# GpSimd takes a second of four products with C in every other group of a selective scan

## Chip, cores and metric

One core of one Trainium2 chip runs the whole program in one launch. The metric is the device time of one execution in microseconds. Before the change three runs took 1963.19, 1964.97 and 1970.44 us; the median is 1964.97.

## What is computed

The reference adds four branches to x (4 batches of 512 tokens of width 512): a quantized two-layer block, a feed-forward with weights from a 16-entry table, a selective scan (Mamba) that is gated by x, and a routed mixture of 32 experts. Only the scan is touched here. Cut to it:

```python
dt = softplus(dt_low @ dt_proj_w + dt_proj_b)     # one value for each channel and step
A = -exp(A_log)                                   # 512 channels x 16 states

def step(state, inp):
    d, b, c, u = inp
    dA = exp(d[..., None] * A)
    state = state * dA + (d * u)[..., None] * b[:, None, :]
    y = einsum('bdn,bn->bd', state, c)
    return state, y
```

For each of 512 channels and 16 states there is a recurrence over 512 steps. Its states are multiplied with C and summed over the 16 states.

## The kernel before

**Stages.** Three stretches follow each other. Up to 345 us: the quantized block, the table lookups that make the feed-forward weights, and the first batch's preparation of the scan. From 345 to about 1103 us: scan and feed-forward, batch by batch. After it: the experts. In the middle stretch the function `weave` (L1052) draws steps from several generators in proportion to their number: the scan of batch b (`scan`, L538), the feed-forward (`lut_ffn`, L352), the preparation of batch b+1 (`prepare`, L481) and the routing of batch b-1 (`route`, L689). This fixes the order in which instructions are written down. A scheduler then orders them for each engine by its own estimate of when inputs and buffers are there, and every engine runs its own list strictly in order.

**Tiles of the scan.** A tile has 128 partitions, 16 states times 8 channels, and 512 steps. For every batch, block of 128 channels `e` (4) and `v` (4) there is one *group* of four tiles, `j` from 0 to 3. So there are 64 groups (16 for each batch) and 256 tiles. I number the groups from 0 to 63; groups with odd number have v = 1 or 3. For each tile:

- SyncE issues a load of `d` (L556; dt and dt times u, spread over 16 states; 4 buffers).
- ScalarE makes the decay, exp(A dt), into a PSUM bank `st` (L561; 3 banks).
- GpSimd makes `dBu`, dt times u times B (L563; 3 buffers).
- VectorE runs the recurrence, `tensor_tensor_scan` (L566 for j = 0, L568 for the others).
- The states are multiplied with C, the second half of the tile `BC`, into a tile `sc` (5 buffers of 128x512 in SBUF).

The last step is where j matters. For j = 0 the scan writes `sc` in SBUF directly, and GpSimd multiplies it in place (L573), written down behind the dBu of j = 2 by `issue_after`, which adds an edge in GpSimd's own order and no wait on another engine. For the other three the scan writes back to its PSUM bank, and VectorE multiplies from there into `sc` (L569).

After the fourth tile, TensorE sums over states with four matmuls (L579), one for each j, into 32 partitions of the bank `py`. Tile 3 goes first, the other three behind it. They free the four `sc` buffers. After four groups VectorE adds the skip term (L589).

**What stands around it.** TensorE's list holds the feed-forward matmuls (L375 gate and up, L391 down) between the groups. VectorE closes each feed-forward chunk with L384 and L385, which free the PSUM bank of that chunk, and adds L391's result to x at L398. `prepare` uses GpSimd for four products of each block (L530, L532, L533, L534) and a store (L535), and VectorE for the convolution (L500, L504) and L529. Layer norms have VectorE statistics (L101, L102, L103), a power on GpSimd (L104) and VectorE's L106, which waits for it. `route` has the matmuls L705 and L710 and the small ones L780, L781 and L819, with VectorE's L782, L801 and L808 beside them.

Of the kernel before, what the change touches and what calls it, by code (L numbers as in the profile page):

```python
# [22 lines left out]
ALU = mybir.AluOpType  # L23
# [36 lines left out]
class Kernel:  # L60
# [477 lines left out]
    def scan(self, mp, b):  # L538


        nc = self.nc
        skip = self.vecs[:, 2, :]
        u = self.u[b]
        BC = mp.tile([P, 2, S], F32, tag="BC", name="BC", bufs=1)
        for g in range(2):
            nc.sync.dma_start(
                out=BC[:, g, :], in_=self.xdbl[b, 1 + g].unsqueeze(1).to_broadcast([NST, CPT, S])
            )
        for e in range(KH):
            py = self.bank("y", f"py{e}")  # L550
            for v in range(4):
                scs = []
                for j in range(4):
                    r0 = e * P + 32 * j + CPT * v
                    d = mp.tile([P, 2, S], F32, tag="d", name="d", bufs=4)
                    nc.sync.dma_start(  # L556
                        out=d, in_=self.dts[b, r0 : r0 + CPT].unsqueeze(0).to_broadcast([NST, CPT, 2, S])
                    )
                    st = self.bank("d", "st")
                    i = (e * 4 + v) * 4 + j  # L560
                    nc.scalar.activation(st, d[:, 0, :], AF.Exp, scale=self.A[:, i : i + 1])  # L561
                    dBu = mp.tile([P, S], F32, tag="dBu", name="dBu", bufs=3)
                    product = nc.gpsimd.tensor_tensor(dBu, d[:, 1, :], BC[:, 0, :], ALU.mult)  # L563
                    sc = mp.tile([P, S], F32, tag="sc", name="sc", bufs=5)
                    if j == 0:
                        nc.vector.tensor_tensor_scan(sc, st, dBu, 0.0, ALU.mult, ALU.add)  # L566
                    else:
                        nc.vector.tensor_tensor_scan(st, st, dBu, 0.0, ALU.mult, ALU.add)  # L568
                        nc.vector.tensor_tensor(sc, st, BC[:, 1, :], ALU.mult)  # L569
                    scs.append(sc)  # L570
                    if j == 2:
                        with self.tc.issue_after(product.ins):
                            nc.gpsimd.tensor_tensor(scs[0], scs[0], BC[:, 1, :], ALU.mult)  # L573
                    if j < 3:
                        yield

                with ExitStack() as behind:
                    for j in (3, 0, 1, 2):
                        y = nc.tensor.matmul(  # L579
                            py[32 * j : 32 * j + 32, :],  # L580
                            lhsT=self.sum_states[:, v, :],
                            rhs=scs[j],
                            start=v == 0,
                            stop=v == 3,
                        )
                        if j == 3:
                            behind.enter_context(self.tc.issue_after(y.ins))
                yield
            nc.vector.scalar_tensor_tensor(  # L589
                u[:, e, :], u[:, e, :], skip[:, e : e + 1], py, ALU.mult, ALU.add  # L590
            )
# [598 lines left out]
```

## Time and profile before

| what | value |
|---|---|
| median of three runs | 1964.97 us (1963.19 to 1970.44) |
| profiled execution, its time | 1967.59 us |
| profiled execution, its span | 1965.8 us |
| mean granted clock of TensorE | 0.933 |
| busy over the span: PE, DVE, ACT, POOL | 85%, 61%, 36%, 51% |
| scan stretch, 345 to 1103 us: PE, DVE, ACT, POOL busy | 660.76, 673.06, 345.83, 503.67 us |
| one product with C: on DVE (L569), on POOL (L573) | 681, 1300 ns |
| one scan (L566, L568) | 1214, 1218 ns |

PE is TensorE's matmul, DVE is VectorE, ACT is ScalarE, POOL is GpSimd and SP is SyncE. The profile is of one execution. Times are microseconds unless marked ns. A row of a group names the source line, the engine, the operation, the tiles written and read, the count, then busy time and the mean of one, then the idle time of the engine just before, with what ended it. A row of the waits reads: who waited, for what, how long in all, how often, and the longest. A row of the timeline has start, duration, engine, line, and in brackets the idle time before it. How much is busy over the whole span is an average over stretches with different limits; the table therefore gives the scan stretch on its own.

### The profile page before, as it was taken

The numbers are of one execution on the slowest core, as the hardware profiler recorded it, in microseconds if no ns is written. First come the engines' busy times: TensorE is split into PE (matmuls) and PEld (weight loads), VectorE is DVE, ScalarE is ACT, GpSimd is POOL, SyncE is SP. The second block draws the span as 40 slices with busy tenths as digits, with TensorE's granted clock in tenths as the row PEclk, the third lists the DMA queues.
The fourth block names the chain that finished last, engine by engine and source line by source line (L and its number), as shares of the span: only waits on it lengthen the run. The fifth ranks groups of instructions, "written<-read, shape, count | busy, mean of one in ns | idle before, by whom it ended". The sixth has DMA issues, their size and how long they took to land. (4 is left out here: it accounts for less than half of the span.)

```text
span 1965.8 us, 25002 instructions
## 1 busy us (share of the span) xinstructions
PE 1667.2 (85%) x8845; PEld 984.2 (50%) x8845; DVE 1192.7 (61%) x2029; ACT 712.7 (36%) x1345; POOL 999.0 (51%) x824
## 2 busy tenths in 40 slices
PE   4778775899889888888799688799999999999980
PEld 2444332556454545454555344455556566556540
DVE  6887864788799979999889634422222233222231
ACT  1554455535443554355433322222222222222210
POOL 3110113768755875478566543556555555555420
PEclk9889986899999998899999799999999999999985
DMA  9524510889887888788789686688888877877656
GB/s 264 140 80 153 182 50 34 221 201 227 211 234 165 208 212 213 165 200 205 207 198 221 189 210 134 165 180 197 176 181 178 185 164 160 180 169 170 111 128 186
DMA packets 187673, 346.69 MB, mean 176 GB/s; under 512 B 41698, under 2 KB 88130, under 8 KB 187540
## 3 DMA queue, kind: packets, MB, share of 16 engines
q1 hardware_dynamic: 147332, 251.96, 48.6%
q0 software_dynamic: 39952, 92.66, 23.7%
q8 instruction: 72, 1.18, 0.3%
q10 hardware_dynamic: 256, 0.39, 0.1%
q14 instruction: 61, 0.50, 0.1%
HBM read 277.08 MB, written 76.32 MB: 180 GB/s over the span
## 5 line engine op out<-in xcount | busy, mean ns | idle before, releaser
L968 POOL DMA_INDIRECT sums<-ey,to x168 | 260.8, 1552 | 311.5 <-DMA sums<-ey,to 123.4
L925 PE MATMUL pg<-exT,egu 128*128 128x320 f32 (+1 forms) x1536 | 402.5, 419 | 15.5 <-DVE eh L943 7.6
L563 POOL TENSOR_TENSOR dBu<-d,BC 128x512 f32<-128x512 f32 x256 | 330.8, 1302 | 112.1 <-DMA d<-dts 79.8
L925 PEld LDWEIGHTS pg<-exT,egu 128*128 128x128 f32 x1536 | 289.2, 191 | 131.8 <-issue 38.0
L568 DVE TENSOR_TENSOR_SCAN st<-st,dBu 128x512 f32<-128x512 f32 x192 | 230.7, 1218 | 29.9 <-POOL dBu L563 25.3
L561 ACT ACTIVATE st<-d,A 128x512 f32<-128x512 f32 x256 | 173.5, 689 | 189.9 <-DVE sc L569 122.1
L375 PE MATMUL pgu<-xT,wg 128*128 128x256 f32 (+1 forms) x704 | 189.4, 412 | 30.6 <-DVE h L385 26.1
L900 POOL DMA_INDIRECT xg<-xln,tokens x168 | 162.0, 964 | 90.8 <-issue 37.9
L942 DVE SCALAR_TENSOR_TENSOR eh<-eh,pg 128x320 f32<-128x320 f32 (+5 forms) x144 | 61.1, 425 | 230.6 <-ACT eh L941 229.3
L954 PE MATMUL po_e<-ed,eh 128*128 128x512 f32 (+1 forms) x336 | 172.9, 633 | 13.2 <-ACT ey L967 6.2
L340 PE MATMUL pw<-oh,lut_t 128*32 128x344 bf16 (+1 forms) x2052 | 127.0, 359 | 65.5 <-DVE oh L334 65.2
L375 PEld LDWEIGHTS pgu<-xT,wg 128*128 128x128 f32 (+1 forms) x704 | 132.3, 198 | 97.3 <-DVE h L385 39.0
L375 PE MATMUL pgu<-xT,wu 128*128 128x256 f32 (+1 forms) x704 | 179.4, 397 | 0.0
L967 ACT ACTIVATE ey<-po_e,gates 128x512 f32<-128x512 f32 (+1 forms) x104 | 68.8, 684 | 303.8 <-PE po_e L958 151.1
L965 DVE TENSOR_SCALAR ey<-po_e,gates 128x512 f32<-128x512 f32 x64 | 45.9, 748 | 209.0 <-PE po_e L958 209.0
L391 PE MATMUL po_f<-wd,h 128*128 128x512 f32 (+1 forms) x352 | 159.8, 610 | 2.6 <-DVE h L385 2.2
L375 PEld LDWEIGHTS pgu<-xT,wu 128*128 128x128 f32 (+1 forms) x704 | 138.5, 199 | 25.8 <-issue 2.9
L569 DVE TENSOR_TENSOR sc<-st,BC 128x512 f32<-128x512 f32 x192 | 127.7, 681 | 19.8 <-PE py L579 18.9
L573 POOL TENSOR_TENSOR sc<-sc,BC 128x512 f32<-128x512 f32 x64 | 83.2, 1300 | 110.0 <-DVE sc L566 83.1
L958 PE MATMUL po_e<-ed,eh 64*128 64x512 f32 (+1 forms) x336 | 114.8, 638 | 0.0
L340 PEld LDWEIGHTS <-lut_t 128*32 128x32 bf16 x2052 | 56.3, 102 | 113.2 <-issue 74.0
L391 PEld LDWEIGHTS po_f<-wd,h 128*128 128x128 f32 (+1 forms) x352 | 68.0, 196 | 86.3 <-issue 80.6
(260 smaller groups left out, 2195.0 us busy)
## 6 DMA issues: line engine op xcount, KB each, us to landing
d<-dts SPq DMA_DIRECT2D x256, 512.0 KB, 6.3
egu<-in_w_gate SPq DMA_DIRECT2D x40, 384.0 KB, 3.8
ix<-idx_b SPq DMA_DIRECT2D x16, 688.0 KB, 5.4
egu<-in_w_up SPq DMA_DIRECT2D x40, 256.0 KB, 5.2
ed<-in_w_down SPq DMA_DIRECT2D x40, 256.0 KB, 4.0
ed<-in_w_down SPq DMA_DIRECT2D x80, 128.0 KB, 4.5
sums<-zero SPq DMA_DIRECT2D x12, 768.0 KB, 6.7
dts<-dt POOLq DMA_DIRECT2D x16, 512.0 KB, 4.5
```

Of the source, the lines that this page charges most:

```text
L340: nc.tensor.matmul(pt[i][32 * c : 32 * c + 32, :step], lhsT=self.lut_t[:, j, g, :], rhs=oh[:, c * n + i * step : c * n + (i + 1) * step], ...
L375: nc.tensor.matmul(pg[:m, j * W : (j + 1) * W], lhsT=w[:, k, c * P : c * P + m], rhs=xT[:, k, :], start=k == 0, stop=k == KH - 1,)
L391: nc.tensor.matmul(po, lhsT=h[:m, c, i * P : (i + 1) * P], rhs=self.wd[:m, c, :], start=c == 0, stop=c == NIC - 1,)
L561: nc.scalar.activation(st, d[:, 0, :], AF.Exp, scale=self.A[:, i : i + 1])
L563: product = nc.gpsimd.tensor_tensor(dBu, d[:, 1, :], BC[:, 0, :], ALU.mult)
L568: nc.vector.tensor_tensor_scan(st, st, dBu, 0.0, ALU.mult, ALU.add)
L569: nc.vector.tensor_tensor(sc, st, BC[:, 1, :], ALU.mult)
L900: nc.gpsimd.indirect_dma_start(out=xg[:m, :], out_offset=None, in_=xln, in_offset=bass.IndirectOffsetOnAxis(ap=tokens[:m, lo + j, col : co ...
L925: nc.tensor.matmul(pg[i][:, :hs], lhsT=w[:, k, i * P : (i + 1) * P], rhs=xT[:, k, z : z + hs], start=k == 0, stop=k == KH - 1,)
L954: nc.tensor.matmul(po[j][:m, :], lhsT=h[:, 0, b : b + m], rhs=wd[:, 0, :], start=True, stop=False)
L958: nc.tensor.matmul(po[j][:m, :], lhsT=h[r : r + R, 1, b : b + m], rhs=wd[r : r + R, 1, :], start=False, stop=True)
L968: nc.gpsimd.indirect_dma_start(out=sums[j], out_offset=bass.IndirectOffsetOnAxis(ap=to[:m, lo + j, col : col + 1], axis=0), in_=y[:m, :], ...
```

## The change

In groups with odd v, `share` is 2: the scans of tiles 0 and 1 both write `sc` directly, and GpSimd multiplies both in place, that of tile 0 behind the dBu of tile 2 as before and that of tile 1 behind the dBu of tile 3. In these groups the summing matmuls begin with tile 1, then 3, 0 and 2. Groups with even v stay as they were. Counted over the program, 32 of the 192 products of VectorE go, and GpSimd has 96 instead of 64.

```diff
             for v in range(4):
-                scs = []
+
+                share = 1 + v % 2
+                products, scs = [], []
                 for j in range(4):
...
-                    product = nc.gpsimd.tensor_tensor(dBu, d[:, 1, :], BC[:, 0, :], ALU.mult)
+                    products.append(nc.gpsimd.tensor_tensor(dBu, d[:, 1, :], BC[:, 0, :], ALU.mult))
                     sc = mp.tile([P, S], F32, tag="sc", name="sc", bufs=5)
-                    if j == 0:
+                    if j < share:
                         nc.vector.tensor_tensor_scan(sc, st, dBu, 0.0, ALU.mult, ALU.add)
                     else:
                         nc.vector.tensor_tensor_scan(st, st, dBu, 0.0, ALU.mult, ALU.add)
                         nc.vector.tensor_tensor(sc, st, BC[:, 1, :], ALU.mult)
                     scs.append(sc)
-                    if j == 2:
-                        with self.tc.issue_after(product.ins):
-                            nc.gpsimd.tensor_tensor(scs[0], scs[0], BC[:, 1, :], ALU.mult)
+                    if 2 <= j < 2 + share:
+                        with self.tc.issue_after(products[j].ins):
+                            nc.gpsimd.tensor_tensor(scs[j - 2], scs[j - 2], BC[:, 1, :], ALU.mult)
                     if j < 3:
                         yield
 
                 with ExitStack() as behind:
-                    for j in (3, 0, 1, 2):
+                    order = (3, 0, 1, 2) if share == 1 else (1, 3, 0, 2)
+                    for j in order:
                         y = nc.tensor.matmul(
...
-                        if j == 3:
+                        if j == order[0]:
                             behind.enter_context(self.tc.issue_after(y.ins))
```

## What I expect

> **What bounds the kernel now.** I read the windows view first, cut where the scan begins (345 us) and ends (1103 us). Its columns are busy time and instructions of each engine, the granted clock, the DMA share and GB/s.
>
> ```profile
> core 0: us, PE busy (x) PEld busy (x) DVE busy (x) ACT busy (x) POOL busy (x), PEclk, DMA share, GB/s
> 345.00:1103.00 758.00, 660.76 (x3028) 404.15 (x3032) 673.06 (x1025) 345.83 (x558) 503.67 (x408) 0.94 0.83 204
> 1103.00:1966.00 863.00, 764.92 (x3089) 450.80 (x3081) 268.55 (x553) 209.55 (x545) 424.67 (x338) 0.95 0.76 171
> ```
>
> The change touches only the first stretch. There two engines are almost full: VectorE 673 of 758 us (89%) and TensorE 661 (87%). GpSimd has 254 us free. The waits of VectorE in that stretch (who waited for whom: us, times, longest) say what its 85 idle us are:
>
> ```profile
> DVE st L568 <- POOL dBu L563: 25.3, 18, 4.2
> DVE sc L569 <- PE py L579: 18.9, 18, 2.6
> DVE ln_off L106 <- POOL ln_rs L104: 12.6, 9, 2.2
> ```
>
> Call a group's instructions b0 to b3 (dBu, L563), S0 to S3 (scans, L566 and L568), M (product with C on VectorE, L569), C (the same on GpSimd, L573) and y (the four summing matmuls, L579). The first wait is an S for its b. The second is M1 for a free sc buffer, which a y of the group before holds. TensorE comes to that y late: in the timeline the median y starts some 3 us after its last M, with feed-forward matmuls before it. One such place, S3 of group 24 and then M1, which waits until the y of group 23 end (640.12 + 1.06 us):
>
> ```profile
> 638.34 1.22 DVE L568 TENSOR_TENSOR_SCAN st<-st,dBu 128x512 f32<-128x512 f32 x1
> 641.20 0.69 DVE L569 TENSOR_TENSOR sc<-st,BC 128x512 f32<-128x512 f32 x1 [1.64 <-PE py L579]
> ```
>
> I followed the waits back by hand from the last M (1102.5 us): where an engine had no gap, to its instruction before; where it had one, to the releaser. Of the 757 us some 340 lie on VectorE, 250 on TensorE, 80 on GpSimd, 55 on DMA (d loads, BC, xln) and 20 on ScalarE. So VectorE's time is worth its full price on less than half of the way. Of the 32 M1 that the change removes (groups with odd v), 16 lie on a VectorE piece (groups 9, 15, 25, 27, 31, 41, 43, 45, 47, 49, 53, 55, 57, 59, 61, 63), the other 16 where TensorE, GpSimd or a transfer decides.
>
> **What is removed and added.** From the page:
>
> ```profile
> L568 DVE TENSOR_TENSOR_SCAN st<-st,dBu 128x512 f32<-128x512 f32 x192 | 230.7, 1218 | 29.9 <-POOL dBu L563 25.3
> L569 DVE TENSOR_TENSOR sc<-st,BC 128x512 f32<-128x512 f32 x192 | 127.7, 681 | 19.8 <-PE py L579 18.9
> L573 POOL TENSOR_TENSOR sc<-sc,BC 128x512 f32<-128x512 f32 x64 | 83.2, 1300 | 110.0 <-DVE sc L566 83.1
> ```
>
> Removed: 32 M1, 32 x 0.681 = 21.8 us of VectorE's records; back to back they overlap a little (two in 1.28 us), so 0.64 each on a full engine, 20.5 us. Added: 32 C1 on GpSimd, 32 x 1.30 = 41.6 us, which raises it from 504 to 545 of 758. S1 now writes SBUF instead of PSUM: L566 does that at 1214 ns against 1218, nothing. Loads, exps and matmuls keep their numbers.
>
> **What the built order adds to the diff.** S1 writes sc itself, so what waited for the sc buffer was M1 and is now S1, a scan earlier. The instruction order of the built kernel shows two answers. In 14 of the 32 groups (3, 5, 7, 9, 13, 21, 25, 29, 37, 41, 45, 53, 57, 61 of 0 to 63) the scheduler puts S1 behind S3: S0 S2 S3 S1 M2 M3; in group 11 it stands between S2 and S3. In the other 17 the order is kept, in several of them with two y of the group before pulled ahead of a block of feed-forward matmuls. C1 mostly stands before the next group's b2, which needs a dBu buffer that S1 frees anyway, so it adds a length but hardly a new wait.
>
> A moved S1 costs in this way. After S0 GpSimd does C0 and b3, and S3 can't start before:
>
> ```profile
> 1027.80 1.27 POOL L573 TENSOR_TENSOR sc<-sc,BC 128x512 f32<-128x512 f32 x1 [0.53 <-DVE sc L566]
> 1029.03 1.26 POOL L563 TENSOR_TENSOR dBu<-d,BC 128x512 f32<-128x512 f32 x1
> ```
>
> S0 of that group ends at 1027.7, b3 at 1030.3, S3 starts at 1030.32: 2.6 us, against 2 x 1.17 = 2.34 for S1 and S2 between. In the moved order only S2 (and what else falls there) fills the 2.6 us, S3 starts no earlier, and S1 (1.17) follows where M1 (0.64) stood: **0.53 us later, not 0.64 sooner**. The same 0.53 is lost where S1, instead of M1, starts at TensorE's gate.
>
> **The sum on the path** (times of before, order of after):
> - kept order on a VectorE piece (groups 27, 43, 49, 59, 63): 5 x 0.64 = 3.2 sooner. Group 55, freed of its gate, gives 0.3 before TensorE's own backlog decides.
> - groups 21 and 37: L398, for which TensorE waits (6.75 us once, as "PE pl L710 <- DVE x L398"), comes ahead of S1; with C1 and the early y behind it, I count 0.7 and 1.9 sooner.
> - moved on a VectorE piece: 45, 53, 61 lose 0.53 each (1.6); 57 0.65; 9 0.9 (a feed-forward product falls behind S3 too); 25 and 41 come out even, since other work is pulled before their gate.
> - groups 15, 31, 47: the last C1 stands ahead of the pow of L104, for which L106 waits 2.2 us each time. It adds 1.24 and saves 0.64: 0.6 lost, three times, 1.8.
> - group 11: C1 joins a GpSimd piece (461 to 484 us): 1.25 lost. Elsewhere GpSimd's own waits for d (79.8 us) and for S0 (83.1 us) hide C1; without that cover all 32 would cost 41.6 us.
> - the 16 off VectorE pieces that are not named: nothing.
>
> Sooner 6.1, later 6.2.
>
> **A rule against it.** One row stands out among VectorE's groups in the scan stretch:
>
> ```profile
> L504 DVE SCALAR_TENSOR_TENSOR u<-u,acc 128x512 f32<-128x512 f32 x12 | 11.5, 955 | 0.1
> ```
>
> Its shortest takes 671 ns in the trace, the mean 955, the longest 1740, which is one GpSimd product more. The Trainium skill ("SBUF — State Buffer", Who interferes with whom) says that such an instruction and a GpSimd one that reads SBUF exclude each other for the whole instruction, and that one with at most one SBUF input does not contend. M1 read PSUM and one SBUF tile, so the rule makes the swap bad: VectorE gives up an uncontended product and GpSimd holds the port 41.6 us more. If every new C1 held such an instruction for half its length, 32 x 0.65 = 21 us. The row says less: the scans keep 1198 to 1234 ns beside GpSimd throughout, and what stands over the shortest is (955-671) x 12 = 3.4 us for L504 and about 1.6 for L604, with some more in L529 and L801; call it 8 us for a GpSimd busy 66%. At 72% it grows by 8/66 x 6 = 0.7 us. I take 0.7, bounded by 0 and 21.
>
> Total: 6.9 later, 6.1 sooner, **0.8 us later**. The profiled execution took 1967.59 (span 1965.8), 2.6 over the median 1964.97. So 1968.4 for it and about 1966 for a median.
>
> **Rivals.**
> 1. *Faster: the freed VectorE time counts.* For it: 89% busy, and TensorE waits for h (26.1 us) and py for sc (10.9), which an earlier VectorE shortens. The 16 on its path give 16 x 0.64 = 10.2, with groups 21 and 37 12.8: 1952. All 32 would give 1944, which the TensorE pieces exclude. Against it: the 14 moved scans.
> 2. *Slower: TensorE waits for C1.* y of an odd group now begins with tile 1, and TensorE is in order: the feed-forward matmuls stand behind it, VectorE's L384 and L385 behind those. At the groups' ends C1 should come near the last M. In groups 11, 27, 29, 43 and 45 prep products (L530 to L534, 1.27 each) stand ahead of it. If C1 comes 3 us after the last M everywhere, the odd groups at which TensorE is less than 3.7 us behind (3, 11, 17, 25, 27, 35, 43, 49, 57, 59, 63) lose 14 us together: 1979. It decides from about 2 us of lateness; at 0 it costs nothing. For it: each b between C1 and its S1 is 1.3 us. Against it: TensorE is 4 to 10 us behind in most odd groups.
> 3. *Slower by the port*, 21 us: 1986. Unlikely by the scans' steady times.
>
> **Chances.** No measurable change 0.62, rival 1 0.14, rivals 2 and 3 and other sums of lost waits 0.24. What a measurement of this kernel can tell from no change is 0.5%, 9.8 us: below 1955.1 or above 1974.8. Each piece is a count of small, alike terms (0.5 to 2 us) of both signs, so the likeliest case alone spans 1957 to 1974. The range reaches to rivals 1 and 2: 1953 to 1980.
>
> **What would show it.** VectorE's busy time in the scan stretch falls by some 20 us and GpSimd's rises by some 41, yet the stretch stays within a few us of 758. Waits of S for dBu grow (25.3 to 35 or more), as do those of L106 for L104 (12.6 by 3 to 4); what waited as M1 for y appears as a scan that waits for y. L569 falls to 160 rows at 681 ns. Wrong would be: a stretch 10 us shorter with unchanged waits (VectorE was the bound), py waiting for the C product on GpSimd by over 10 us (rival 2), or scans or L504 longer on average (rival 3).

## The result and the profile after

The changed kernel took **1991.30 us** (median of 4 runs, 1990.54 to 1992.80), beside 1964.08 us for the kernel before on the same chip. The medians are 27 us apart. The ratio of the record is 1.0126, with a 95% interval of 1.0105 to 1.0148: 25 us slower, where no measurable change was forecast, and outside the range.

The windows view of the kernel after, cut where its scan ends (columns as in the forecast):

```profile
core 0: us, PE busy (x) PEld busy (x) DVE busy (x) ACT busy (x) POOL busy (x), PEclk, DMA share, GB/s
345.00:1134.00 789.00, 685.55 (x3032) 409.19 (x3032) 662.14 (x993) 344.73 (x558) 538.63 (x439) 0.93 0.80 196
1134.00:1990.00 856.00, 763.19 (x3081) 452.38 (x3081) 268.61 (x553) 209.61 (x545) 424.31 (x338) 0.95 0.77 173
```

The whole loss lies in the scan. The window of before, in the forecast, ends ahead of the last group's y; up to the end of that y (1104.5 us) TensorE has 662.2 us and VectorE 673.2. Between equal ends the stretch grew by 29.5 us (759.5 to 788.9). What follows it was untouched and took 861 us before and 856 after; over the traces of all kernels here it took 853 to 869. VectorE has 32 products fewer and is 11 us less busy. **TensorE is 23 us busier with the same matmuls**, and the other 6 us are added idle time on it.

The costliest groups of the page after (lines from L554 on stand two or three further down than before; L570 and L568 are the scans, L571 the product with C on VectorE, L575 that on GpSimd):

```profile
L575 POOL TENSOR_TENSOR sc<-sc,BC 128x512 f32<-128x512 f32 x96 | 124.4, 1296 | 116.6 <-DVE sc L568 93.9
L570 DVE TENSOR_TENSOR_SCAN st<-st,dBu 128x512 f32<-128x512 f32 x160 | 192.5, 1217 | 61.3 <-POOL dBu L565 46.1
L571 DVE TENSOR_TENSOR sc<-st,BC 128x512 f32<-128x512 f32 x160 | 105.7, 677 | 18.0 <-PE py L582 17.3
```

Scan and product have kept their lengths (1217 and 677 ns against 1218 and 681). What grew on VectorE is the waiting. The waits of the same kernel, in the scan stretch:

```profile
DVE st L570 <- POOL dBu L565: 46.1, 32, 3.6
...
PEld py L582 <- POOL sc L575: 17.7, 7, 4.8
...
PE py L582 <- POOL sc L575: 15.0, 6, 4.6
...
DVE ln_off L106 <- POOL ln_rs L104: 9.8, 9, 2.2
...
DVE sc L568 <- PE py L582: 8.7, 11, 2.3
```

The wait of the scans for dBu grew as foreseen (25.3 to 46.1), and 8.7 us of the waits for y are now those of scans, as foreseen too. The one for L104 fell (12.6 to 9.8) where it was to grow. The second and third line are new, and are one wait seen twice, at the weight load and at the matmul: **TensorE stands still at a summing matmul for GpSimd's product**. In the trace 14.6 us of it lie in four places. 2.75 us from 608.8, 4.56 from 816.3 and 3.37 from 1021.0 us are in groups 21, 37 and 53, all three among the 14 with a moved scan; 3.91 from 1126.9 are in group 63, the last, whose order of scans is unchanged; there TensorE was idle before as well, for 5.78 us until VectorE's last product. This is the first of them, in the timeline:

```profile
606.42 1.23 DVE L570 TENSOR_TENSOR_SCAN st<-st,dBu 128x512 f32<-128x512 f32 x1 [1.23 <-POOL dBu L565]
...
608.19 0.66 PE L708 MATMUL pt_r<-ident,xn_r 128*128 128x128 f32 x4
...
608.38 0.68 DVE L398 TENSOR_TENSOR x<-x,po_f 128x512 f32<-128x512 f32 x1
...
608.98 1.22 DVE L568 TENSOR_TENSOR_SCAN sc<-st,dBu 128x512 f32<-128x512 f32 x1
...
610.27 1.27 POOL L575 TENSOR_TENSOR sc<-sc,BC 128x512 f32<-128x512 f32 x1 [0.57 <-DVE sc L568]
...
611.60 1.48 PE L582 MATMUL py<-sc,sum_states 128*32 128x512 f32 x2 [2.75 <-POOL sc L575]
```

Read it from below. TensorE is in order, and its list has the y of tile 1 ahead of the routing's matmuls (L713). These could start at 609.5 us: L398 has by then read the PSUM bank that they write (609.1; it is one of two banks that L391, L708 and L713 share), and ScalarE has their input (L710, 609.5). The y waits until 611.6 for C1, C1 for S1, and S1 stands behind S3, which itself waited 1.23 us for b3, and behind L398. Tile 1 is first in y, but its product is the last thing of its group to be ready.

This wait is not all added time. In groups 21 and 37 the kernel before was idle at the same place, 3.39 and 6.75 us in front of the routing's matmul, until L398 freed the bank. Its waits had this line, which the kernel after does not have:

```profile
PE pl L710 <- DVE x L398: 10.1, 2, 6.8
```

The other loss of TensorE is seen in the rest of group 21's y (629.20), in those of group 22, in two parts, and in those of group 23. Each y makes two records, so x8 are four matmuls:

```profile
629.20 1.06 PE L582 MATMUL py<-sc,sum_states 128*32 128x512 f32 x6
630.66 0.66 PE L366 MATMUL pt_x<-ident,xn 128*128 128x128 f32 x4 [0.40 <-ACT xn L111]
632.28 1.05 PE L582 MATMUL py<-sc,sum_states 128*32 128x512 f32 x4 [0.97 <-DVE sc L571]
...
636.92 1.05 PE L582 MATMUL py<-sc,sum_states 128*32 128x512 f32 x4
...
648.77 1.06 PE L582 MATMUL py<-sc,sum_states 128*32 128x512 f32 x8
```

**Four y side by side take 1.06 us, three take 1.06, and two 1.05.** A group whose y are parted by other matmuls pays that for each part. The order built for the kernel before parts 4 of the 64 groups, that for the change 15. The time with a y on TensorE went from 75.9 to 93.6 us, 17.7 of the 23 us above. Eleven more parts at 1.05 us are 11.6 of them. The other 6 are y that ran at half the granted clock, of which there are more after:

```profile
562.50 1.92 PE L582 MATMUL py<-sc,sum_states 128*32 128x512 f32 x4 [0.42 <-DVE sc L571]
```

The windows view has a granted clock of 0.50 for these 1.92 us and of 1.00 for the 1.06 us at 648.77. In all traces here the record of the granted clock has only 1.0 and 0.5 in this stretch. Half of the time in which TensorE is busy at 0.5 can thus be counted as lost by the clock, and the rest of its busy time as work. So counted, from the trace of before to that of after, with the places bounded by the ends of the groups' y:

| place | longer, us | work | lost at half clock | idle |
|---|---|---|---|---|
| ends of batches: from group 11 to 15, 27 to 31, 43 to 48, 55 to 60 | 20.9 | 1.9 | 12.2 | 6.8 |
| groups 20 to 23, 36 to 39, 52 to 55 | 8.2 | 6.6 | 0.4 | 1.3 |
| the rest of the stretch | 0.4 | 2.7 | -0.5 | -2.0 |
| all, 345 us to the last y | 29.5 | 11.2 | 12.1 | 6.1 |

The work is the parted y. Around groups 21, 37 and 53 these, not the idle time, make most of the loss against the kernel before. The larger loss lies at the ends of the batches, where GpSimd prepares the next batch, and most of it is TensorE at half clock. Each side is one execution, and no run sets the clock by itself; what lowers it is left open.

### The profile page after: what moved, and what is told of

It is laid out like the page before. It is cut to its first block, busy times and chain, and to the rows that moved or that the text cites. A ratio compares the mean times of both kernels' runs of the same rounds, so it can differ in the third digit from the quotient of the medians.

```text
span 1989.5 us, 24948 instructions
## 1 busy us (share of the span) xinstructions
PE 1689.4 (85%) x8836; PEld 990.8 (50%) x8845; DVE 1181.7 (59%) x1997; ACT 711.8 (36%) x1345; POOL 1033.7 (52%) x856
## 5 line engine op out<-in xcount | busy, mean ns | idle before, releaser
L570 DVE TENSOR_TENSOR_SCAN st<-st,dBu 128x512 f32<-128x512 f32 x160 | 192.5, 1217 | 61.3 <-POOL dBu L565 46.1
L375 PE MATMUL pgu<-xT,wg 128*128 128x256 f32 (+1 forms) x704 | 194.3, 421 | 26.0 <-DVE h L385 23.7
L575 POOL TENSOR_TENSOR sc<-sc,BC 128x512 f32<-128x512 f32 x96 | 124.4, 1296 | 116.6 <-DVE sc L568 93.9
L957 PE MATMUL po_e<-ed,eh 128*128 128x512 f32 (+1 forms) x336 | 172.3, 632 | 13.6 <-ACT ey L970 6.2
L375 PE MATMUL pgu<-xT,wu 128*128 128x256 f32 (+1 forms) x704 | 175.0, 389 | 0.0
L391 PE MATMUL po_f<-wd,h 128*128 128x512 f32 (+1 forms) x352 | 161.7, 615 | 5.2 <-DVE h L385 3.5
L568 DVE TENSOR_TENSOR_SCAN sc<-st,dBu 128x512 f32<-128x512 f32 x96 | 116.4, 1213 | 11.0 <-PE py L582 8.7
L571 DVE TENSOR_TENSOR sc<-st,BC 128x512 f32<-128x512 f32 x160 | 105.7, 677 | 18.0 <-PE py L582 17.3
L391 PEld LDWEIGHTS po_f<-wd,h 128*128 128x128 f32 (+1 forms) x352 | 68.4, 197 | 90.6 <-issue 82.1
```

Source lines behind the costliest of these rows:

```text
L375: nc.tensor.matmul(pg[:m, j * W : (j + 1) * W], lhsT=w[:, k, c * P : c * P + m], rhs=xT[:, k, :], start=k == 0, stop=k == KH - 1,)
L391: nc.tensor.matmul(po, lhsT=h[:m, c, i * P : (i + 1) * P], rhs=self.wd[:m, c, :], start=c == 0, stop=c == NIC - 1,)
L575: nc.gpsimd.tensor_tensor(scs[j - 2], scs[j - 2], BC[:, 1, :], ALU.mult)
L957: nc.tensor.matmul(po[j][:m, :], lhsT=h[:, 0, b : b + m], rhs=wd[:, 0, :], start=True, stop=False)
```

## The experiments

At first there were three theories. *S*: tile 1 first in y parts the summing matmuls. *G*: 32 more products on GpSimd cost something although it has idle time. *M*: the 14 scans moved behind the fourth. Ratios are to the kernel before on the same chip; 0.001 is 2 us. "Parted" and "moved" count groups in the built order. What is told of a place in a trace comes from one execution.

| run | what | parted | moved | ratio (95%) |
|---|---|---|---|---|
| after | the change | 15 | 14 | 1.0126 (1.0105 to 1.0148) |
| b_y1first | before, with the new order of y | 14 | 0 | 1.0068 (1.0044 to 1.0092) |
| b_poolx | before, 32 idle products behind b3 | 4 | 0 | 1.0076 (1.0051 to 1.0101) |
| b_pool1 | before, 32 idle products behind b1 | 4 | 0 | 1.0025 (1.0012 to 1.0038) |
| e_noC1 | change without C1 | 15 | 14 | 1.0034 (1.0019 to 1.0050) |
| e_y3first | change, old order of y | 6 | 20 | 1.0068 (1.0042 to 1.0095) |
| e_keep | change, S1's place kept | 12 | 0 | 1.0082 (1.0054 to 1.0110) |
| e_keep_y3 | the same, old order of y | 2 | 0 | 1.0080 (1.0052 to 1.0108) |
| e_keep_y3_noC1 | the same without C1 | 2 | 0 | 1.0066 (1.0047 to 1.0084) |
| e_fix4 | change, tile 1 last in y in four groups | 9 | 17 | 1.0069 (1.0045 to 1.0093) |
| b_sc6 | before, six sc buffers | 8 | 0 | 0.9988 (0.9973 to 1.0002) |
| e_sc6_y3_noC1 | six, old order of y, without C1 | 7 | 0 | 0.9975 (0.9956 to 0.9994) |
| e_sc6_y3 | six, old order of y | 7 | 0 | 1.0031 (1.0019 to 1.0043) |
| e_sc6 | change, six | 16 | 0 | 1.0054 (1.0040 to 1.0067) |
| e_sc6_m14 | six, the 14 scans moved by hand | 16 | 14 | 1.0129 (1.0097 to 1.0162) |
| e_sc6_m14_fix4 | the same, tile 1 last in y in four groups | 13 | 14 | 1.0065 (1.0040 to 1.0090) |
| e_sc6_y3_8 | six, old order, C1 in 8 groups | 8 | 0 | 1.0023 (1.0010 to 1.0037) |
| e_sc6_y3_24 | six, old order, C1 in 24 groups | 7 | 0 | 0.9973 (0.9957 to 0.9989) |

### One part of the change at a time

**b_y1first**: the kernel before, with only the order of y.

```diff
-                    for j in (3, 0, 1, 2):
+                    for j in ((3, 0, 1, 2), (1, 3, 0, 2))[v % 2]:
...
-                        if j == 3:
+                        if j == (3, 1)[v % 2]:
```

> The kernel before, with one thing of the change: in groups with odd v the four summing matmuls are written down with tile 1 first (1, 3, 0, 2). No product moves. In its built order 14 groups have their four matmuls parted by other matmuls, against 4 before and 15 after the change. Theory S (parting costs TensorE: four together take 1.06 us side by side, each part alone takes 1.06 again): TensorE's busy time in the scan stretch rises by 12 to 18 us and the time by 8 to 18 us, to about 1972 to 1982. Theory G (GpSimd: its extra products, and the scans that wait for dBu, are the cost): within 3 us of before, 1962 to 1968. Theory M (scans moved behind the fourth): no scan is moved here, so as G.

1.0068, 13 us slower, with TensorE's y at 94.5 us against 75.9. S is real, in a kernel that has nothing else of the change. But the new order does more than part. The y of tile 1 stands ahead of the routing's matmul here too and waits for VectorE's product, 4.56, 7.01 and 2.17 us in groups 21, 37 and 53, with no scan moved and nothing new on GpSimd; the 10.1 us of waits for L398 are gone. From group 20 to 23, 36 to 39 and 52 to 55 this trace is 10.7 us longer than that of before, of 11.0 in all.

**b_poolx**: the kernel before, with a product of B and C into a scratch tile that nobody reads (its room is made as that of the sixth buffer below).

```diff
+                    if j == 3 and v % 2:
+                        with self.tc.issue_after(product.ins):
+                            extra = mp.tile([P, S], F32, tag="extra", name="extra", bufs=1)
+                            nc.gpsimd.tensor_tensor(extra, BC[:, 0, :], BC[:, 1, :], ALU.mult)
```

> The kernel before, with 32 more products on GpSimd, one behind the dBu of the fourth tile of each group with odd v, that read B and C and write a tile nobody reads; VectorE keeps all its 192 products. (One routing tile shares a buffer with another to make room.) The computation is unchanged. Theory G (GpSimd's 1.27 us each lands in front of dBu products that scans wait for): waits of scans for dBu rise from 25.3 by 10 us or more and the time by 10 to 25 us, 1975 to 1990. Theories S and M: GpSimd is 66% busy in the stretch and its waits for d and for scans hide it: within 4 us of before.

1.0076, 15 us. GpSimd was 66% busy in the stretch, and work on it that nothing waits for still costs more than a third of its own length (32 x 1.27 = 41 us). VectorE's wait for L104 rose from 13.8 to 18.7 us, cut at 1140 us for both. G is real too, though not by the waits for dBu that I had named: these rose from 25.3 to 27.9 us only. Of the 17.5 us by which the stretch is longer in the trace, 15.4 lie at the ends of the batches, and 14.3 are TensorE busy at half clock.

**e_noC1** and **e_y3first**: the change without GpSimd's second product, and the change with the old order of y.

```diff
-                    if 2 <= j < 2 + share:
+                    if j == 2:
```

> The changed kernel without the second product on GpSimd: tile 1 of groups with odd v is not multiplied with C at all, which leaves 32 of 256 products out. Scans that are moved and matmuls that are parted stay as in the change: 14 moved, 15 parted. Theory G: the cost goes with the product, 1965 or below. Theory S: parted matmuls stay, TensorE's busy time in the stretch keeps its 20 us more; 1980 to 1988. Theory M (a scan that starts where a product started is 0.53 us later, and the fourth scan waits for its dBu): as S, 1978 to 1990, with waits of scans for dBu still above 40 us.

```diff
-                    order = (3, 0, 1, 2) if share == 1 else (1, 3, 0, 2)
+                    order = (3, 0, 1, 2)
```

> The changed kernel with the summing matmuls in the old order (3, 0, 1, 2) in all groups. In its built order only 6 groups are parted (15 in the change), but 20 scans of tile 1 stand behind the fourth scan (14 in the change). Theory S: most of the loss goes, 1966 to 1976. Theory M: it grows, 1992 to 2002. Theory G: it stays, 1986 to 1994.

The first takes away three quarters of the loss (1.0034, with all 14 scans moved and 15 groups parted), the second nearly half (1.0068, with even 20 scans moved). None of the three theories had 1971 us for the first or 1977 for the second in its range. In neither trace does a y wait for GpSimd; in e_noC1 the y of tile 1 waits 7.6 us for S1 itself, in groups 21, 37, 53 and 63. So the parts don't add up: a late S1, C1 behind it and tile 1 first in y are one chain, which is shorter without C1 and does not form without the new order of y.

### The sixth buffer

If S1 is moved because the scheduler has no free sc buffer for it, a sixth buffer ends the moves. Its room in SBUF comes from a tile of the routing (oh) that now shares the room of xT.

```diff
-                    sc = mp.tile([P, S], F32, tag="sc", name="sc", bufs=5)
+                    sc = mp.tile([P, S], F32, tag="sc", name="sc", bufs=6)
...
-        oh = rp.tile([P, TPB * TOPK, NE], BF16, tag="oh", name="oh", bufs=1)
+        oh = rp.tile([P, TPB * TOPK, NE], BF16, tag="xT", name="oh", bufs=1)
```

**e_sc6** is the change with it, **e_sc6_y3** has the old order of y besides, **b_sc6** is the control.

> The change with six buffers instead of five under the tag of sc (the one-hot tile of the routing shares a dead tile's room to pay for it). In the built order no scan is moved behind the fourth any more (14 were), 16 groups have their y matmuls parted (15), and all C1 stand ahead of the next group's b0. M (moved scans) expects most of the 27 us to go: about 1970, with the VectorE waits on dBu back from 46 to near 27. S and G (parted matmuls and GpSimd's extra products) expect them to stay, as neither is touched: S + G from the runs so far is 11 + 15 less what VectorE saves, so 1975 to 1990, with the time of the y matmuls still near 93 us.

> The same with the old order of y (fourth first) in all groups: no scan moved, 7 groups parted (4 before the change). It is the change with GpSimd's products alone. If S and M were all of the loss, it is at or below the kernel before: 1950 to 1964, with VectorE's saved products counting. If GpSimd's 32 products cost what they cost when added for nothing (15 us), and VectorE's saved time gives back a part, 1966 to 1979, with the y matmuls' time near 80 us. G expects the second.

> Control: the kernel before with six buffers under the tag of sc; 8 groups parted (4 before), no scan moved. All theories expect 1961 to 1969: four more parted groups cost 4 us at most by S, and a buffer more removes at most VectorE's 19 us of waits for the y matmuls, of which the part on the way is not known. Well below 1960 would say that the buffers were a bound of their own, and that the two runs with six must be read against this one.

With six buffers no scan is moved, and the change costs 11 us instead of 25; the control lies at 0.9988. The same 32 idle products at another place are **b_pool1** (`j == 1` in the edit of b_poolx):

> The kernel before with the same 32 extra products on GpSimd (B with C into a tile that nobody reads) as in the run that cost 15 us, now behind the second dBu of the odd groups and not behind the fourth. If the price is that of the place (preparation and the next group's first dBu queued behind the extra product), it changes: here the third and fourth dBu are queued behind it, and the second scan's cover runs beside it; less than 8 us expected, or with waits for dBu on VectorE clearly over 28 us. If it is the price of GpSimd working at all (a lower granted clock for TensorE, 0.922 against 0.933 then), it stays at 12 to 18 us with a clock near 0.92 and feed-forward matmuls some 9 us longer.

5 us instead of 15. GpSimd did the same work, and TensorE's granted clock in the profile was 0.937 (0.922 in b_poolx, 0.933 before). Over all runs of b_poolx the clock was 0.926 on average, over those of b_pool1 0.932 and over those of before 0.931. So GpSimd's work has no fixed price, and does not lower the clock by itself: its place has a price, and in b_poolx most of that is paid at half clock.

### The moved scans, and what they cost by

**e_keep**: five buffers, S1's place kept by an edge in VectorE's order. **e_keep_y3** has the old order of y besides, and **e_keep_y3_noC1** no C1 either.

```diff
-                        nc.vector.tensor_tensor_scan(sc, st, dBu, 0.0, ALU.mult, ALU.add)
+                        first = nc.vector.tensor_tensor_scan(sc, st, dBu, 0.0, ALU.mult, ALU.add)
                     else:
-                        nc.vector.tensor_tensor_scan(st, st, dBu, 0.0, ALU.mult, ALU.add)
+                        with self.tc.issue_after(first.ins):
+                            nc.vector.tensor_tensor_scan(st, st, dBu, 0.0, ALU.mult, ALU.add)
```

> The change with its five buffers, but with the second scan's place written out: the third and fourth scans are issued behind it. In the built order no scan is moved (14 were), all C1 stand ahead of the next group's b0 (15 stood behind), 12 groups parted (15). If the 18 us that the sixth buffer gave back came from the scans' order (M), this comes to 1970 to 1977, as with six buffers. If they came from the waits for a free buffer on the chip, it stays at 1985 to 1995, with VectorE's waits for the y matmuls over the 26 us of before-to-change (17.3 and 8.7).

> The kept order of scans with the old order of y in every group: nothing moved, 2 groups parted (4 before the change). It is the change with its GpSimd products and VectorE's saved time alone, at five buffers. If these gain what they were meant to (rival 1 of the forecast), 1950 to 1960; if GpSimd's product costs as much as it saves, 1962 to 1970 (1969.6 with six buffers, 7 parted).

> The same without the second tile's product with C in the odd groups at all (32 of the 256 products left out, so the summed states of these tiles lack C): what VectorE's 20.4 us of saved products are worth alone. If they are worth most of their time, 1943 to 1952, and the difference to the run with C1 on GpSimd is C1's price. If VectorE's time hardly counts, 1958 to 1964, and C1's price is what the run with it lies above that. I expect 1950 (clock and waits as in the kernel before, VectorE some 20 us less busy in the stretch).

All three times missed what I expected; only e_keep's mark, VectorE's waits for y over 26 us, came true (38.4). Without any move the change still costs 16 us, and even without C1 and with only 2 groups parted it costs 13, where I had looked for a gain. In e_keep TensorE still waits 12.9 us for C1, in groups 21, 37 and 53 as before, and in 63: S1 stands ahead of S2 again, but in group 21 both stand behind L398 (S1 starts at 604.6 us, the y of tile 1 at 607.2). The waits of e_keep_y3_noC1 (its profiled execution is among its longest, 1991.97 us, with a median of 1978.34) name the other cause:

```profile
DVE sc L568 <- PE py L583: 22.9, 21, 3.0
...
DVE sc L572 <- PE py L583: 13.6, 10, 2.8
```

A scan that writes sc takes its buffer a scan earlier than the product did, and with five buffers it then waits for the y of the group before, 22.9 us in all. With the products' 13.6 VectorE waits 36.5 us for y, against 18.9 in the kernel before. The scans' wait is absent from the trace of **e_sc6_y3_noC1** below, which differs mainly by the buffer, and is at 0.9975; the products wait 24.3 us there. So the shortage is real, and the move was an answer to it. Without C1 it seems the better one: 1.0034 in e_noC1, with 15 groups parted, against 1.0066, with intervals that just overlap. A part of this loss too is the clock: 0.925 on average over the 17 runs of e_keep_y3_noC1, 0.932 over the 22 of before beside them.

**e_sc6_m14** sets the 14 scans behind the fourth by hand where six buffers would not need it:

```diff
+MOVED = (3, 5, 7, 9, 13, 21, 25, 29, 37, 41, 45, 53, 57, 61)
...
-                    if j < share:
+                    if j == 1 and b * 16 + e * 4 + v in MOVED:
+                        late = (sc, st, dBu)
+                    elif j < share:
...
-                        nc.vector.tensor_tensor_scan(st, st, dBu, 0.0, ALU.mult, ALU.add)
+                        fourth = nc.vector.tensor_tensor_scan(st, st, dBu, 0.0, ALU.mult, ALU.add)
+                        if j == 3 and b * 16 + e * 4 + v in MOVED:
+                            with self.tc.issue_after(fourth.ins):
+                                nc.vector.tensor_tensor_scan(*late, 0.0, ALU.mult, ALU.add)
```

> Six buffers, with the second scan set behind the fourth by hand in the same 14 groups as in the change; C1 then stands behind the next group's b0 in 14. 16 groups parted, as with six buffers alone (1973.2), so that only the move is added. M expects 1985 to 1995 (the change: 1991.3), with the waits of the scans on dBu from 27 up to 40 or more. If the buffer itself was the cause, 1971 to 1977.

The whole loss is back: 1.0129 against 1.0054. But the mechanism I had given M is not what the trace shows: the scans' waits for dBu hardly grew (27.8 to 29.3 us). The view of the tile py on TensorE, in e_sc6_m14, shows what did grow (us, times):

```profile
its engine sat idle before it (us, times) until:
  POOL sc L582: 20.8, 4
```

and the first of the four in the timeline, where the y that waited then runs at half clock as well:

```profile
614.28 1.92 PE L589 MATMUL py<-sc,sum_states 128*32 128x512 f32 x2 [6.98 <-POOL sc L582]
```

In e_sc6 the same line had 4.5 us, 4.1 of them in the last group. (Its profiled execution, 1961.85 us, is the shortest of six with a median of 1973.22; that of e_sc6_m14, 2001.99, is the longest of six with a median of 1992.50. So the two traces tell the places, not the size.) In e_sc6_m14 this last one is there too, and 16.7 us are new: 7.0, 6.9 and 2.8 in groups 21, 37 and 53. Two waits for L398 at these places, 6.0 us in e_sc6, are gone. **e_sc6_m14_fix4** leaves the 14 scans where they are and changes the order of y in four groups; **e_fix4** does this in the change itself:

```diff
                     order = (3, 0, 1, 2) if share == 1 else (1, 3, 0, 2)
+                    if b * 16 + e * 4 + v in (21, 37, 53, 61):
+                        order = (3, 0, 2, 1)
```

> The kernel with six buffers and the 14 scans moved by hand (1992.5), with the y matmul of the second tile set last instead of first in four groups only: 21, 37, 53 and 61, the four in which the trace has TensorE idle for C1 on GpSimd (7.0, 6.9, 2.8 and 4.1 us, 20.8 in sum). All 14 scans stay moved, and C1 stands behind the next group's b0 in 14 as before; 13 groups parted instead of 16. If the move's price is TensorE waiting in order for a late C1 (rival 2 of the forecast), 1969 to 1978, with hardly any wait of the y matmuls for GpSimd. If the price is VectorE's waits for dBu and the moved scans themselves, 1986 to 1995.

> The change itself (five buffers) with the same edit in the same four groups. The built order then moves 17 scans instead of 14, with 18 C1 behind the next group's b0 instead of 15, and parts 9 groups instead of 15. TensorE's waits for C1 in the change were 14.6 us in these four groups. Rival 2 expects 1972 to 1979 for it, though more is moved; if moved scans cost by themselves, it is at 1985 or above.

Both expectations put the fourth wait into group 61. That was misread: it is in group 63, which the edit does not touch, and the y of group 61 were not parted. The edit decides in 21, 37 and 53. On this chip the kernel before took 1968.64 us and these two 1980.99 and 1980.49; by ratio, both runs come to where the waiting of TensorE put them (1977 and 1978 us for 1964): from 1.0129 to 1.0065 (12.6 us), and from 1.0126 to 1.0069 (11.2 us) though 17 scans are now moved. The same view of e_sc6_m14_fix4:

```profile
its engine sat idle before it (us, times) until:
...
  POOL sc L584: 4.1, 1
```

The three waits are gone, and that of group 63 is left. In groups 21 and 37 TensorE is idle in front of the routing's matmul instead, until L402 (L398 of before) frees its bank:

```profile
PE pl L724 <- DVE x L402: 8.9, 2, 5.0
```

So of 16.7 us of waiting only half came back as idle time, and 12.6 us as time. Three groups fewer are parted, which at the half to 1.3 us that one costs elsewhere is 1.5 to 4 us of the 12.6. The traces agree on the place: from e_sc6_m14 to e_sc6_m14_fix4, from group 20 to 23, 36 to 39 and 52 to 55 are 12.9 us shorter, 6.5 by less idle time, 4.2 by the clock and 2.2 by less work. So some 9 to 11 us of the move's price (14.7 us, e_sc6 to e_sc6_m14) are this one mechanism in three groups. The differences of ratios behind this have intervals of 6 to 8 us to each side.

### What GpSimd's product costs by itself

**e_sc6_y3_noC1** is e_sc6_y3 with `if j == 2:` as in e_noC1.

> Six buffers, the old order of y, and the second tile's product with C in the odd groups left out (32 of 256 products, so these tiles' states are summed without C): nothing moved, 7 parted, as in the run with that product on GpSimd (1969.6). What VectorE's saved 20.4 us are worth where the buffers don't bind: if they count, 1943 to 1953, and GpSimd's product costs the 17 to 27 us between. If VectorE's time hardly sets the end, 1957 to 1963 (1961.0 with six buffers and all products on VectorE), and the product on GpSimd costs 7 to 13 us by itself.

0.9975. Against b_sc6 (0.9988) the 20 us that VectorE saves are worth 2.6 us, with intervals that overlap: next to nothing. Against e_sc6_y3 (1.0031) the 32 products on GpSimd cost 11 us. From group to group, these two traces part in four places, towards the end of each batch (12 to 16, 28 to 31, 44 to 48, 56 to 60; 3.6 to 5.3 us each, 18 in all, of which 12 to 13 are regained between them; at the end the two traces are 5.6 us apart). One of them in the timeline of e_sc6_y3, groups 12 and 13:

```profile
485.78 1.26 POOL L565 TENSOR_TENSOR dBu<-d,BC 128x512 f32<-128x512 f32 x1
487.00 1.26 POOL L530 TENSOR_TENSOR lost<-dt,lost 128x512 f32<-128x512 f32 x1
487.07 1.23 DVE L570 TENSOR_TENSOR_SCAN st<-st,dBu 128x512 f32<-128x512 f32 x1 [1.49 <-POOL dBu L565]
...
495.78 1.23 DVE L570 TENSOR_TENSOR_SCAN st<-st,dBu 128x512 f32<-128x512 f32 x1 [1.80 <-POOL dBu L565]
496.29 1.28 POOL L575 TENSOR_TENSOR sc<-sc,BC 128x512 f32<-128x512 f32 x1
497.52 1.26 POOL L565 TENSOR_TENSOR dBu<-d,BC 128x512 f32<-128x512 f32 x1
498.75 1.26 POOL L575 TENSOR_TENSOR sc<-sc,BC 128x512 f32<-128x512 f32 x1
498.82 1.23 DVE L570 TENSOR_TENSOR_SCAN st<-st,dBu 128x512 f32<-128x512 f32 x1 [1.50 <-POOL dBu L565]
```

From 477.5 to 503.7 us GpSimd has no gap at all (in the rows each start is the start before it plus 1.2 us): the preparation of the next batch (L530 to L535), dBu and the products with C follow each other, and three of the scans wait 1.5 to 1.8 us for their dBu. GpSimd has no room there, and each product more on it is 1.2 us. The last two runs split the 32 products by that:

```diff
+BUSY = (13, 15, 29, 31, 45, 47, 57, 59)
...
-                share = 1 + v % 2
+                share = 1 + (v % 2 and b * 16 + e * 4 + v in BUSY)
```

> Six buffers, old order of y, and the second product with C on GpSimd in eight odd groups only: 13, 15, 29, 31, 45, 47, 57 and 59, beside the preparation of the next batch and at its end, where the run with all 32 slipped against the run without them (from group to group: +4.9 us in 12 to 16, +5.3 in 28 to 31, +3.6 in 44 to 48, +4.4 in 56 to 60). The other 24 have it on VectorE again. If the price of GpSimd's product (11 us for 32) is one of place, these eight carry it: 1.002 to 1.006 of before. If every product costs alike, a quarter: 0.999 to 1.002.

> The complement: on GpSimd in the other 24 odd groups, on VectorE in those eight. Nothing moved, 7 groups parted. If place is the price: as without GpSimd's products at all, 0.996 to 0.9995 of before (1957 to 1963), which would beat both kernels. If every product costs alike, 1.001 to 1.003.

Against b_sc6 the eight groups cost 7 us on their own (1.0023), all 32 cost 8.4 (1.0031), and **the other 24 cost nothing** (0.9973, with `not in`). The two parts sum to less than the whole, within their intervals. All this is with six buffers and nothing moved. The version with the 24 beats both kernels: 0.27% faster than the one before (interval 0.9957 to 0.9989). The control b_sc6 (0.9988) is not clearly slower, so a gain of the 24 products over the buffer alone is not shown.

## Why the prediction was wrong

**Where it looked.** It followed the chain of the kernel *before* and weighed the change at that chain's pieces. Its 6.1 us sooner and 6.9 later cancelled. The loss came from chains that the change itself made, at places to which the sum gave a fraction of a us. That its terms nearly cancelled says nothing for them.

1. *"A moved S1 costs in this way ... 0.53 us later."* This step failed first. The 14 moves and their reason (no free sc buffer) were read rightly from the built order, but I followed S1 only to VectorE's next instruction, not to its consumers: C1, then the y that the change sets first, then all that stands behind that y on TensorE. For groups 21 and 37 the sum has "0.7 and 1.9 sooner", for 53 0.53 later. Measured in the change: TensorE idle for 2.75, 4.56 and 3.37 us for C1, the first two in place of 10.1 us for L398, and the y parted. From group 20 to 23, 36 to 39 and 52 to 55 the change came out 2.1, 1.0 and 5.1 us later. 11 to 13 us of time come back when the order of y is changed in these and one group more.
2. *Rival 2, "TensorE waits for C1".* The mechanism was right, and its own mark ("py waiting for the C product on GpSimd by over 10 us") was passed with 15.0. Its places were wrong, but for the last group. It looked for C1 late behind preparation products on GpSimd (11, 27, 29, 43, 45); what made C1 late was a late S1, moved, or behind L398 (e_keep). The 3.9 us of the last group cost nothing, as TensorE had been idle there before. "TensorE is 4 to 10 us behind in most odd groups" held for most, and failed in three.
3. *"Loads, exps and matmuls keep their numbers."* Their numbers, not their time. That tile 1 goes first in y was put at nothing, without a reason. In the traces of before and after, the parted y are 11.2 us more work for TensorE. With tile 1 first, 10 groups more are parted, and that costs 13 us in the kernel before (b_y1first); 9 groups more cost 4.5 us with six buffers (e_sc6_y3 to e_sc6).
4. *"Elsewhere GpSimd's own waits ... hide C1."* True in 24 groups and not in eight. The cover was read from sums over the stretch (79.8 and 83.1 us of waits, 66% busy), where the question was whether GpSimd had a gap beside the preparation. It had none. I had priced three of these groups, by L104; that wait fell from 12.6 to 9.8 us. By place this is where most of the change's loss lies: 20.9 of 29.5 us at the ends of the batches, to which the sum gave some 2 us. C1 is not all of it. Against before, these places are 12.6 us longer without C1 (e_noC1), 5.7 with S1's place kept (e_keep) and 3.0 with six buffers and the moves (e_sc6_m14), so that five buffers, moves and C1 make it together.
5. *"The same 0.53 is lost where S1, instead of M1, starts at TensorE's gate."* Too small, where S1 keeps its place: with five buffers that costs some 18 us (e_keep_y3_noC1 1.0066, e_sc6_y3_noC1 0.9975), of which the sixth buffer gives 2.4 in the kernel before too. The built order avoided most of it in the change by moving S1; the two prices stand for each other and may not be added.

**What held.** VectorE's saved time is worth little: 2.6 us measured, where the moves and the buffer don't interfere, with intervals that overlap. Rival 1 found nothing of its 12 us. The row was weighed rightly against the rule of the Trainium skill ("SBUF — State Buffer", Who interferes with whom) on instructions that exclude each other: scans and products kept their times, and the five exposed VectorE groups (L504, L529, L604, L801 and L808 of before) went from 74.3 to 74.9 us, with two of L604's 16 lying outside the same window after. That this is within 2 us of the 0.7 is in part luck: L801 grew by 9.7 us (1532 to 2345 ns each) and L808 fell by 6.2. In the pair that differs by the 32 products alone (e_sc6_y3_noC1, e_sc6_y3) the five groups have 70.1 and 73.7 us. Neither is near the 21. (The longest L504 is 1.07 us above the shortest, less than one GpSimd product of 1.30.)

**One account of the 25 us**, in the order of the six-buffer runs: VectorE's saved products -2.6; GpSimd's products +11 (those in the eight places alone 7, against b_sc6); parted y +4.5; the moved scans +14.7, of which 9 to 11 are TensorE waiting in three groups. The sum, 27.6 from b_sc6 on, ends at 1.0129, where the change itself is at 1.0126. Each step has an uncertainty of 3 to 7 us. With five buffers the parts depend on each other, and I have no such ladder for them. How much of each step is the half clock, and what lowers it, stays open: e_sc6_m14 to e_sc6_m14_fix4 raised it from 0.928 to 0.931 over all runs. VectorE became less busy by 11 us only, with 32 products of 0.68 us gone: the single times of its instructions sum to 17.5 us less (products 22.4 less, L801 9.8 more, L808 6.2 less), and 7 us of overlap between neighbours are gone.

## What to carry to other kernels

When a result is made later or on another engine, follow it through every in-order queue to the end, to who reads it and what is queued behind that reader: the tile that is ready last, set first, holds up every matmul behind it, and set last it came 11 to 13 us cheaper here, in three groups. Look for room on a helper engine at the place where the work would stand, not in its share over the stretch: of 32 products 24 were free (with six buffers), and eight, at a place without a gap, cost 7 us. Before a wait in a trace is counted as a loss, see what stood at the same place before: the new waits for C1 in two groups, 7.3 us, stood in place of 10.1 us of others. And an instruction that writes a shared buffer earlier takes it earlier, which here cost more than the instruction saved.

## What the runs showed of the hardware

Summing matmuls into different 32-partition parts of one bank run beside each other: one alone (1.04 us, group 21 in e_keep) takes as long as two (1.05), three or four (1.06, at 512 columns in f32). What separated them in TensorE's order here, a transpose of 0.66 us for instance, made the next part pay in full. At a granted clock of 0.50 a part takes 1.9 us (two at 562.50 us in the kernel after, one at 614.28 in e_sc6_m14). I had the 1.06 us before me in the trace as the length of a group's y, and did not ask what it is for a part of them.
